# A graph network's first pass: gathered rows copied to PSUM by ScalarE, ends of edge lists found by one-hots, theta from rows in SBUF

## The chip, the cores and the metric

The kernel runs on one core of one Trainium2 chip. The metric is the time of one execution on the device in microseconds; of several runs the median is given. Engines are named as the profile names them: PE is TensorE's matmul and PEld its weight load, DVE is VectorE, ACT is ScalarE, POOL is GpSimd, SP is SyncE (here it only starts DMAs).

## The reference

Two graph layers with residuals and layer norms work on 6250 nodes of 256 features and 100000 edges, which are sorted by destination. All arithmetic is float32.

```python
def _L0_gnn_ref(x, src, dst, theta_w, theta_b, phi_w, phi_b):
    x_src = x[src]
    x_dst = x[dst]
    theta_x = (x_dst - x_src) @ theta_w.T + theta_b
    phi_x = x_src @ phi_w.T + phi_b
    e = jax.nn.relu(theta_x + phi_x)
    out = jax.ops.segment_max(e, dst, num_segments=x.shape[0])
    return jnp.where(jnp.isfinite(out), out, 0.0)

def _L1_gnn_ref(x, he, src, dst, W_in, b_in, W_u0, b_u0, W_u1, b_u1, W_ro, b_ro):
    hv = x @ W_in + b_in
    deg = jax.ops.segment_sum(jnp.ones_like(dst, jnp.float32), dst, num_segments=n)
    has_in = (deg > 0)[:, None]
    for W, b in ((W_u0, b_u0), (W_u1, b_u1)):
        m = jnp.concatenate([hv[src], he], axis=-1)
        m = jax.nn.relu(m @ W + b)
        msg = jax.ops.segment_max(m, dst, num_segments=n)
        hv = jnp.where(has_in, msg + hv, hv)
    return jax.nn.relu(hv @ W_ro + b_ro)

x = _layernorm(x + _L0_gnn_ref(x, src, dst, ...), axis=-1)
x = _layernorm(x + _L1_gnn_ref(x, edge_attr_64, src, dst, ...), axis=-1)
```

Since theta of a destination is the same for all its edges, the first layer needs the largest value of `x_src @ (phi - theta)` over a node's edges, to which theta of the node is added afterwards.

## The kernel before, in words

There are three passes over the edges: pass 0 is the first layer, passes 1 and 2 are the two rounds of the second. Each runs the same function `sweep(r)`. The edges, in reverse order of destination, are laid out as 14 blocks; in a block each of the 128 partitions (lanes) has 56 consecutive edges (54 in the last block), so a pass has 782 steps (`FS`), and one step takes one edge of each lane.

In a step GpSimd gathers 128 rows of 256 values from a table in HBM (`sources`, L790), 16 steps ahead of its use. In passes 1 and 2 TensorE adds the edge features (`pair`, L825) in PSUM, and VectorE adds the gathered rows to them, two steps at a time (L1030). VectorE then takes the running maximum along each lane (the scan, L1043): `cur = max(min(prev, lim), row)`, where `lim` is very negative at an edge that starts another destination. In pass 0 both inputs of the scan, `prev` and `row`, lie in SBUF, except in 40 steps (two of each eight in the first 160): for these, rows of x are gathered raw and multiplied on the core (`raw_turn`, `raw_pair`), and the scan reads PSUM. Every eight steps SP writes the scanned rows to a buffer `S` in HBM (L1051). At a block's end `over_lanes` carries the last row of each lane over to the lanes below (L836 to L857).

Nodes are handled in 49 tiles of 128, from the last to the first. `node(t, g, b)` puts a tile's work into slots, that is, behind given steps: at slot g GpSimd gathers the tile's rows from `S` by `end_i` (`rows`, L870), after the writes of `S` that were issued since the gather before it; at b-3 and b-2 VectorE and TensorE pick the rows that carry over (`picks` L882, `carried` L889, tile `v`); from b on come the additions, the layer norm, the products for the next table and the write of that table (pass 0: `first_a` to `first_g`, L904 to L928; later passes: `next_a` to `next_d` or `last_d` to `last_g`, L931 to L958). Which blocks a tile touches is fixed by `SPAN`, one to three blocks for each tile, 73 tile-block pairs in all.

All of this is one order written out by hand (`tc.manual_schedule()`): each engine takes its instructions in the order in which the code issues them, and waits on semaphores for the others. The slots only set that order. Tiles follow each other at a distance of `gap` slots, 6, 4 and 6 in the three passes.

Pass 0 has two more jobs before its nodes. `count` (L710 to L721) counts in-degrees: for each eight steps VectorE makes one-hot matrices `ol` and `oh` in bf16 (a single buffer each) and TensorE multiplies and sums them in PSUM (`hist`), one call every three steps from step 28 on. `ends_a` and `ends_b` turn the counts into `has` and `end_i`. So pass 0's first node gathers come at slot 324 and its first node steps at slot 344; after that a tile follows every six slots to slot 602, and the last five wait for their blocks. Theta is computed per tile at slots 8i+8 to 8i+21 (i = 0 for the last tile): SP loads the transposed rows (`x_in`, L894), TensorE multiplies (`theta`, L768 with `wt`), VectorE adds the bias and writes `h_sb` (`theta_out`, L900). The rows of x themselves are loaded to `x_sb` in seven DMAs at slots 160 to 208.

Of the kernel before, what the change touches and what calls it, by code (L numbers as in the profile page):

```python
# [17 lines left out]
P = 128  # L18
# [46 lines left out]
WIDE = max(sum(a <= b <= z for a, z in SPAN) for b in range(NB))  # L65

# [7 lines left out]
def gather_raw(nc, x, x_sb, s_r, i):  # L74

    nc.gpsimd.indirect_dma_start(out=x_sb[:, i, :], out_offset=None, in_=x,
                                 in_offset=bass.IndirectOffsetOnAxis(ap=s_r[:, i:i + 1], axis=0))
# [382 lines left out]
def gnn_kernel(  # L460
# [13 lines left out]
    above = const.tile([P, P], F32)  # L474
    nc.vector.tensor_scalar(above, jmp, 0.0, None, OP.is_gt)
# [4 lines left out]
    col = const.tile([P, P], BF16)  # L480
    nc.vector.tensor_copy(col, col_i)
# [30 lines left out]
    lo = const.tile([P, FS], BF16)  # L512
    hi = const.tile([P, FS], BF16)
    with tc.manual_schedule(), tc.tile_pool(name="pro", bufs=2) as pro, \
# [6 lines left out]
        for i in range(SOON):  # L521
            gather_raw(nc, x, x_sb, s_r, i)
        zero = pro.tile([1, D], F32, name="zero", bufs=1)
# [14 lines left out]
        def check():  # L538
# [15 lines left out]
            alike = BLOCKS.count(BLOCKS[0])  # L554
# [9 lines left out]
            nc.vector.tensor_scalar(bits, d_s, P - 1, None, OP.bitwise_and)  # L564
            nc.vector.tensor_copy(lo, bits)
            nc.vector.tensor_scalar(bits, d_s, 7, None, OP.arith_shift_right)
            nc.vector.tensor_copy(hi, bits)
# [29 lines left out]
def in_order(ctx: ExitStack, tc: tile.TileContext, g):  # L597
# [9 lines left out]
    table, ident, above, every, col, col_f = (g[n] for n in ("table", "ident", "above", "every", "col", "col_f"))  # L607
    whole, lim, lo, hi, s_s, fd, pd, ld, nd = (g[n] for n in ("whole", "lim", "lo", "hi", "s_s", "fd", "pd", "ld", "nd"))
    heT, xTn, xn, out = (g[n] for n in ("heT", "xTn", "xn", "out"))
    s_e, head, x, x_sb, wd, s_r = (g[n] for n in ("s_e", "head", "x", "x_sb", "wd", "s_r"))  # L610
    part = g["part"]
# [6 lines left out]
    has = one.tile([P, NT], F32, name="has")  # L618
# [3 lines left out]
    ones = one.tile([P, NT], F32, name="ones")  # L622
    nc.vector.memset(ones, 1.0)
# [72 lines left out]
    hist = psum.tile([P, 512], F32, tag="v", name="hist", bufs=1)  # L696

    none = one.tile([P, NT], BF16, name="none")
    nc.vector.memset(none, 0.0)
    half = (NG + 1) // 2  # L700
    low = []
    for i in range(2):
        low.append(psum.tile([P, 512], F32, tag="he", name="low", bufs=3))
        n = min(half * K, FS - i * half * K)
        nc.scalar.copy(low[i][:, :n], lo[:, i * half * K:i * half * K + n])

    def count(c):
        k = min(K, FS - c * K)
        ol = work.tile([P, K, P], BF16, name="ol", bufs=1)
        nc.vector.tensor_tensor(ol[:, :k, :], col.unsqueeze(1).to_broadcast([P, k, P]),  # L710
                                low[c // half][:, c % half * K:c % half * K + k].unsqueeze(2).to_broadcast([P, k, P]), OP.is_equal)
        b = max(i for i in range(NB) if FIRST[i] <= c * K)
        tiles = [t for t in range(NT) if SPAN[t][0] <= b <= SPAN[t][1]]
        t0, w = tiles[0], len(tiles)
        oh = work.tile([P, K, WIDE], BF16, name="oh", bufs=1)
        nc.vector.tensor_tensor(oh[:, :k, :w], col[:, t0:t0 + w].unsqueeze(1).to_broadcast([P, k, w]),  # L716
                                hi[:, c * K:c * K + k].unsqueeze(2).to_broadcast([P, k, w]), OP.is_equal)
        if c == 0:
            nc.tensor.matmul(hist[:, :NT], ol[:, 0, :], none, start=True, stop=False)
        for j in range(k):  # L720
            nc.tensor.matmul(hist[:, t0:t0 + w], ol[:, j, :], oh[:, j, :w], start=False,  # L721
                             stop=(c == NG - 1 and j == k - 1))

    cnt, incl, end = (one.tile([P, NT], F32, name=n) for n in ("cnt", "incl", "end"))
    sums = []

    def ends_a():
        nc.vector.tensor_copy(cnt, hist[:, :NT])
        ps = psum.tile([P, 512], F32, tag="pr", name="sums")
        nc.tensor.matmul(ps[:, :NT], above, cnt, start=True, stop=True)  # L730
        nc.tensor.matmul(ps[:, 64:64 + NT], every, cnt, start=True, stop=True)
        sums.append(ps)
        nc.vector.tensor_scalar(has, cnt, 0.0, None, OP.is_gt)

    def ends_b():
        lower, total = sums[0][:, :NT], sums[0][:, 64:64 + NT]
        nc.vector.tensor_tensor_scan(incl, ones, total, 0.0, OP.mult, OP.add)
        nc.vector.tensor_sub(end, total, incl)
        nc.vector.tensor_sub(end, end, lower)
        nc.vector.tensor_add(end, end, has)  # L740
        nc.vector.tensor_scalar(end, end, float(E - 2), 0.0, OP.add, OP.max)
        nc.vector.tensor_copy(end_i, end)
# [22 lines left out]
    def times(aT, w, n, tag="pr"):  # L765
        ps = psum.tile([P, 512], F32, tag=tag, name="prod", bufs=3 if tag == "he" else 2)
        for k in range(2):
            nc.tensor.matmul(ps[:, :n], aT[:, k, :], w[:, k, :], start=(k == 0), stop=(k == 1))  # L768
        return ps
# [349 lines left out]
```

## Time and profile before

| | |
|---|---|
| median of 6 runs | 4001.15 us (3986.94 to 4031.39) |
| the profiled execution | 4020.05 us |
| its span, first to last instruction | 4018.2 us |
| PE busy | 1875.5 us, 47% of the span |
| DVE busy | 2118.2 us, 53% |
| ACT busy | 238.1 us, 6% |
| POOL busy | 2390.3 us, 59% |
| mean granted TensorE clock | 0.684 |
| data moved over the span | 739.39 MB, 184 GB/s |

A group in the profile's tables reads: line, engine, operation, out<-in by the program's names, shapes, count, then after a bar the busy time and the mean duration in ns, and after the next bar the idle time of that engine just before the group and what ended most of it. "remote" is a wait whose end the profile cannot put down to an instruction, "issue" one that it cannot explain. A line of the waits has the engine and what it was about to do, whom it waited for, and then the total in us, the number of times and the longest.

### The profile page before, as it was taken

What the parts mean: (1) busy time and instruction counts of PE and PEld (TensorE: products, weight loads), DVE (VectorE), ACT (ScalarE), POOL (GpSimd) and SP (SyncE); (2) the same over time, 40 slices, a digit from 0 to 9 for tenths busy, and PEclk for the clock granted to TensorE, in tenths of its full rate; (3) what the DMA queues carried; (4) which work ended last, traced back from release to release, by engine and by line L of the source; (5) the groups of instructions that cost most, each with busy time, mean ns of one, the idle gap of its engine ahead of it and who ended that gap; (6) DMA issues with size and microseconds to landing.
All of it is one profiled execution on the core that took longest, in us unless ns stands there. A gap on an engine that the chain in (4) does not pass through costs nothing. (4 is left out here: it accounts for less than half of the span.)

```text
span 4018.2 us, 21650 instructions
## 1 busy us (share of the span) xinstructions
PE 1875.5 (47%) x4631; PEld 830.8 (21%) x4631; DVE 2118.2 (53%) x4750; ACT 238.1 (6%) x618; POOL 2390.3 (59%) x2500
## 2 busy tenths in 40 slices
PE   5552223555520354555445554455544544444455
PEld 4341111221200122222112211122222222111111
DVE  1465554554543355455445555445655655555555
ACT  1000001111100000000000000000000000000000
POOL 5456566666666565556655665655555556666663
PEclk8665556666555677777767767667777777777766
DMA  6456555555555565555555665555555555555554
GB/s 236 152 191 212 180 175 177 179 170 173 174 196 173 164 209 179 179 178 184 178 170 188 201 205 175 195 176 195 184 177 176 185 180 188 189 184 186 193 192 163
DMA packets 241821, 739.39 MB, mean 184 GB/s; under 512 B 52485, under 2 KB 95858, under 8 KB 204434
## 3 DMA queue, kind: packets, MB, share of 16 engines
q0 software_dynamic: 119664, 326.92, 27.3%
q1 hardware_dynamic: 69568, 337.85, 22.6%
q10 hardware_dynamic: 52450, 73.16, 5.5%
q8 instruction: 39, 0.64, 0.1%
q14 instruction: 100, 0.82, 0.1%
HBM read 404.56 MB, written 333.17 MB: 184 GB/s over the span
## 5 line engine op out<-in xcount | busy, mean ns | idle before, releaser
L790 POOL DMA_INDIRECT run<-table,s_s x2258 | 2163.4, 958 | 1258.1 <-issue 662.0
L825 PE MATMUL hp<-whe,hT 128*128 128x512 f32 x1564 | 1020.4, 750 | 802.0 <-DVE run L1043 391.5
L1043 DVE SCALAR_TENSOR_TENSOR run<-run,lim,hp 128x256 f32<-128x256 f32 x1573 | 753.8, 479 | 57.4 <-remote 10.7
L1030 DVE TENSOR_TENSOR hp<-hp,run 128x512 f32<-128x512 f32 x782 | 543.5, 695 | 366.4 <-remote 182.6
L825 PEld LDWEIGHTS hp<-whe,hT 128*128 128x128 f32 x1564 | 303.0, 225 | 1351.1 <-DVE run L1043 730.9
L1043 DVE SCALAR_TENSOR_TENSOR run<-run,lim 128x256 f32<-128x256 f32 x731 | 351.5, 481 | 153.8 <-remote 51.2
L870 POOL DMA_INDIRECT m<-S,end_i x147 | 141.4, 962 | 312.8 <-DMA S<-run 208.0
L889 PE MATMUL v<-cs,pick 128*128 128x256 f32 (+1 forms) x438 | 167.2, 502 | 156.8 <-issue 54.6
L931 DVE TENSOR_TENSOR m<-m,v 128x256 f32<-128x256 f32 x98 | 40.6, 414 | 328.5 <-remote 207.0
L768 PE MATMUL prod<-wcat,aT 128*128 128x512 f32 x196 | 176.6, 1054 | 55.2 <-issue 41.6
L710 DVE TENSOR_TENSOR ol<-col,low 128x1024 bf16<-128x1024 bf16 x98 | 118.8, 1213 | 104.6 <-remote 85.8
L721 PE MATMUL hist<-oh,ol 128*128 128x8 bf16 (+7 forms) x782 | 34.8, 167 | 279.0 <-DVE oh L716 184.5
L768 PE MATMUL prod<-wro,aT 128*128 128x256 f32 x196 | 81.4, 556 | 170.2 <-ACT aT L762 89.8
L889 PEld LDWEIGHTS v<-cs,pick 128*128 128x128 f32 x438 | 102.2, 253 | 265.9 <-issue 211.6
L947 DVE TENSOR_TENSOR m<-prod,bro 128x256 f32<-128x256 f32 x49 | 20.8, 425 | 234.5 <-remote 103.9
L768 PE MATMUL prod<-wu,aT 128*128 128x256 f32 x196 | 74.4, 516 | 117.8 <-issue 88.5
L760 PE MATMUL tp<-ident,x_sb 128*128 128x128 f32 x98 | 32.1, 429 | 158.3 <-DVE x_sb L755 68.3
L760 PE MATMUL tp<-ident,h_sb 128*128 128x128 f32 x196 | 48.3, 335 | 121.6 <-DVE h_sb L935 50.1
L926 DVE TENSOR_TENSOR new<-prod,b 128x256 f32<-128x256 f32 x49 | 20.8, 424 | 156.1 <-PE prod L768 89.0
L932 ACT ACTIVATE m<-m,has 128x256 f32<-128x256 f32 x98 | 49.7, 507 | 865.5 <-DVE m L931 368.0
L721 PEld LDWEIGHTS <-ol 128*128 128x128 bf16 x782 | 36.3, 104 | 304.6 <-DVE ol L710 214.9
L762 ACT COPY aT<-tp 128x256 f32<-128x256 f32 x147 | 54.7, 372 | 742.4 <-remote 309.4
(131 smaller groups left out, 1389.0 us busy)
## 6 DMA issues: line engine op xcount, KB each, us to landing
S<-run SPq DMA_DIRECT2D x291, 1024.0 KB
hT<-in_heT ACTq DMA_DIRECT2D x196, 256.0 KB
run<-table,s_s POOLq DMA_INDIRECT x2258
table<-new ACTq DMA_DIRECT2D x98, 128.0 KB
xg<-in_xTn SPq DMA_DIRECT2D x7, 896.0 KB
xT<-in_xTn SPq DMA_DIRECT2D x49, 128.0 KB
x_sb<-in_xn SPq DMA_DIRECT2D x7, 896.0 KB
out<-new ACTq DMA_DIRECT2D x48, 128.0 KB
```

Of the source, the lines that this page charges most:

```text
L710: nc.vector.tensor_tensor(ol[:, :k, :], col.unsqueeze(1).to_broadcast([P, k, P]), low[c // half][:, c % half * K:c % half * K + k].unsquee ...
L721: nc.tensor.matmul(hist[:, t0:t0 + w], ol[:, j, :], oh[:, j, :w], start=False, stop=(c == NG - 1 and j == k - 1))
L760: nc.tensor.transpose(tp[:, k * P:(k + 1) * P], a[:, k * P:(k + 1) * P], ident)
L762: nc.scalar.copy(aT.rearrange("p k e -> p (k e)"), tp[:, :2 * P])
L768: nc.tensor.matmul(ps[:, :n], aT[:, k, :], w[:, k, :], start=(k == 0), stop=(k == 1))
L790: nc.gpsimd.indirect_dma_start(out=runs[s // K][:, s % K, :], out_offset=None, in_=table[r][:SPARE + 1, :] if early else table[r], in_offs ...
L825: nc.tensor.matmul(hp[i], hT[c][:, q, :], whe[r - 1].rearrange("p s f -> p (s f)"), start=True, stop=not early)
L870: i = nc.gpsimd.indirect_dma_start(out=o["m"], out_offset=None, in_=S_r[:P * (FIRST[SPAN[t][1]] + BLOCKS[SPAN[t][1]]), :], in_offset=bass. ...
L889: nc.tensor.matmul(o["v"][:, :N1], p, cs[:, blk % KEPT, :N1], start=(blk == SPAN[t][0]), stop=(blk == SPAN[t][1]))
L932: nc.scalar.activation(o["m"], o["m"], AF.Relu, scale=has[:, t:t + 1])
L1030: nc.vector.tensor_add(sums, sums, two)
L1043: nc.vector.scalar_tensor_tensor(cur, prev, lim[:, s:s + 1], row, OP.min, OP.max)
```

## The change

Pass 0 is changed in four ways, and the later passes in one.

- Each pair of gathered rows is copied by ScalarE into a PSUM buffer (`bring`, three buffers with tag "he", which theta and the copies for counting used before), two pairs ahead of the scan; the scan reads its row from PSUM in all steps. The raw rows' products go to the same buffers.
- In-degrees are no longer counted. `ends(t)` finds for each tile, at slot g-12, which lane of which block holds the node's last edge (two VectorE steps make a one-hot over lanes and nodes for each tile-block pair, TensorE multiplies it with the lanes' destinations in `lane`), and VectorE counts in PSUM how many of the lane's edges precede. From that come `end_i`, and `keeps`, which takes the place of `has`: very large for a node with edges and very negative for one without.
- Theta is no longer computed ahead into `h_sb`. A tile's rows in `x_sb` are transposed (`x_turn`, slot b-6) and multiplied (`theta`, b-4); the bias is added by one more matmul with the identity, and the sum is read from PSUM in `first_b`. The seven loads of `x_sb` come at slots 2 to 138, and the raw rows are stored in `x_sb` in reverse, so that the places are free in time.
- With no counting to wait for, nodes begin as soon as their block is scanned: the first tile's rows are gathered at slot 56 and its steps begin at slot 76. The distance in pass 0 is 8 slots.
- In all passes, adding, cutting off below zero and masking are two fused VectorE steps or one, where VectorE and ScalarE took turns before, and the later steps of a node follow one or two slots earlier.

```diff
 def gather_raw(nc, x, x_sb, s_r, i):
-    nc.gpsimd.indirect_dma_start(out=x_sb[:, i, :], out_offset=None, in_=x,
+    nc.gpsimd.indirect_dma_start(out=x_sb[:, RAW - 1 - i, :], out_offset=None, in_=x,
...
+        nc.gpsimd.iota(n_i, pattern=[[P, NT]], base=1, channel_multiplier=1)
+        nc.gpsimd.iota(at_i[:, :alike], pattern=[[P * BLOCKS[0], alike]], base=-1, channel_multiplier=BLOCKS[0])
...
-            nc.vector.tensor_scalar(bits, d_s, P - 1, None, OP.bitwise_and)
-            nc.vector.tensor_copy(lo, bits)
-            nc.vector.tensor_scalar(bits, d_s, 7, None, OP.arith_shift_right)
-            nc.vector.tensor_copy(hi, bits)
+            nc.vector.tensor_copy(n1, n_i)
+            nc.vector.tensor_copy(fn[:, 0, :], fd)
+            nc.vector.tensor_copy(fn[:, 1, :], nd)
+            nc.vector.tensor_copy(lane[:, :, BLOCKS[0]:], at_i.unsqueeze(2))
...
-    def count(c):
...
-    def ends_a():
...
-    def ends_b():
...
+    def ends(t):
+        b0, b1 = SPAN[t]
+        top = work.tile([P, NB], F32, name="top")
+        nc.vector.tensor_scalar(top[:, b0:b1 + 1], fn[:, 0, b0:b1 + 1], float(-P * t), None, OP.add)
+        ps = psum.tile([P, 512], F32, tag="tp", name="ends")
+        for b in range(b0, b1 + 1):
+            own = work.tile([P, P], F32, tag="pick", name="here", bufs=4)
+            nc.vector.tensor_scalar(own, col_f, fn[:, 1, b:b + 1], float(-P * t), OP.subtract, OP.is_gt)
+            nc.vector.scalar_tensor_tensor(own, col_f, top[:, b:b + 1], own, OP.is_le, OP.mult)
+            nc.tensor.matmul(ps[:, :BLOCKS[0] + 1], own, lane[:, b, :], start=b == b0, stop=b == b1)
+        found = work.tile([P, 2, BLOCKS[0]], F32, name="found")
+        num = work.tile([P, 2], F32, name="num")
+        for i, op in enumerate((OP.is_ge, OP.is_equal)):
+            nc.vector.scalar_tensor_tensor(found[:, i, :], ps[:, :BLOCKS[0]], n1[:, t:t + 1], every[:, :BLOCKS[0]], op,
+                                           OP.mult, accum_out=num[:, i:i + 1])
+        nc.vector.tensor_scalar(end_i[:, t:t + 1], ps[:, BLOCKS[0]:BLOCKS[0] + 1], num[:, 0:1], 0.0, OP.add, OP.max)
+        nc.vector.tensor_scalar(keeps[:, t:t + 1], num[:, 1:2], 0.0, 2.0 * BIG, OP.is_gt, OP.mult)
+        nc.vector.tensor_scalar(keeps[:, t:t + 1], keeps[:, t:t + 1], -BIG, None, OP.add)
...
-    def times(aT, w, n, tag="pr"):
+    def times(aT, w, n, more=None):
...
+        if more is not None:
+            nc.tensor.matmul(ps[:, :n], ident, more, start=False, stop=True)
...
-        def raw_pair(i):
-            aT = rT.pop(i)
-            hp[i * K // 2] = psum.tile([P, 512], F32, tag="pr", name="hp")
+        def bring(i):
+            hp[i] = psum.tile([P, 512], F32, tag="he", name="hp", bufs=3)
+            if raw(2 * i) is None:
+                c, q = divmod(i, K // 2)
+                nc.scalar.copy(hp[i], runs[c][:, 2 * q:2 * q + 2, :].rearrange("p s f -> p (s f)"))
+                return
+            aT = rT.pop(raw(2 * i) // 2)
...
-            def x_in():
-                o["xT"] = work.tile([P, K // 2, P], F32, tag="hT", name="xT", bufs=4)[:, :2, :]
-                nc.sync.dma_start(o["xT"], xTn[:, :, t * P:(t + 1) * P])
+            def x_turn():
+                o["xT"] = turned(x_sb[:, t, :])
             def theta():
-                o["h"] = times(o["xT"], th, D, tag="he")
-            def theta_out():
-                nc.vector.tensor_add(h_sb[:, t, :], o["h"][:, :D], tb)
+                o["h"] = times(o["xT"], th, D, more=tb)
...
             def first_b():
-                nc.vector.tensor_add(o["m"], o["m"], h_sb[:, t, :])
-                nc.scalar.activation(o["m"], o["m"], AF.Relu, scale=has[:, t:t + 1])
-            def first_c():
-                nc.vector.tensor_add(o["m"], o["m"], x_sb[:, t, :])
+                nc.vector.scalar_tensor_tensor(o["m"], o["m"], keeps[:, t:t + 1], o["h"][:, :D], OP.min, OP.add)
+                nc.vector.scalar_tensor_tensor(o["m"], o["m"], 0.0, x_sb[:, t, :], OP.max, OP.add)
...
             def next_a():
-                nc.vector.tensor_max(o["m"], o["m"], o["v"][:, :D])
-                nc.scalar.activation(o["m"], o["m"], AF.Relu, scale=has[:, t:t + 1])
+                nc.vector.scalar_tensor_tensor(o["m"], o["m"], keeps[:, t:t + 1], o["v"][:, :D], OP.min, OP.max)
...
             if r == 0:
-                i = NT - 1 - t
-                at(8 * i + 8, x_in)
-                at(8 * i + 20, theta)
-                at(8 * i + 21, theta_out)
+                at(max(2, g - 12), ends, t)
+                at(b - 6, x_turn)
+                at(b - 4, theta)
...
-                for i, f in ((0, first_a), (1, first_b), (3, first_c), (4, first_d), (6, first_e), (7, first_f),
-                             (9, first_g)):
+                for i, f in ((0, first_a), (1, first_b), (2, first_d), (4, first_e), (5, first_f), (7, first_g)):
...
-                for i, f in ((0, next_a), (2, next_b), (3, next_c)):
+                for i, f in ((0, next_a), (0, next_b), (1, next_c)):
...
-            for c in range(NG):
-                at(3 * c + 28, count, c)
-            begin = 3 * NG + 30
-            at(begin - 2, ends_a)
-            at(begin - 1, ends_b)
-        gap = (6, 4, 6)[r]
+        gap = (8, 4, 6)[r]
...
+                    if s == 0:
+                        bring(1)
+                    if s + 4 < FS:
+                        bring(s // 2 + 2)
                     sums = hp.pop(s // 2)
```

## The prediction

> **What bounds the kernel now.** I read the page first, then a table of busy time by stretch, then VectorE's groups and GpSimd's waits inside the stretches of pass 0. The cuts come from the scan instructions in order of time (one per step): step 0 starts at 97.5 us, step 616 at 1121.7, step 781 ends at 1350.6; passes 1 and 2 run to 2683 and 4018. The span is 4018.2 us, the execution 4020.05, so 1.9 us lie around it.
>
> ```profile
> core 0: us, PE busy (x) PEld busy (x) DVE busy (x) ACT busy (x) POOL busy (x), PEclk, DMA share, GB/s
> ...
> 97.00:604.00 507.00, 184.95 (x1215) 136.87 (x1214) 290.99 (x584) 14.87 (x34) 282.72 (x292) 0.56 0.55 182
> 604.00:1121.00 517.00, 258.88 (x457) 104.84 (x456) 260.64 (x769) 72.43 (x194) 329.19 (x336) 0.61 0.52 172
> 1121.00:1350.00 229.00, 31.19 (x53) 12.57 (x53) 92.17 (x212) 8.09 (x25) 156.16 (x158) 0.52 0.55 185
> ```
>
> I call these stretches I (counting, theta, raw rows), II (most nodes) and III (the rest). No engine is over 68% busy, so waits set the pace. The firm floor is GpSimd: a gather is 0.95 us busy and 0.30 us of issue, 1.25 us. Stretch III is near it: 158 gathers x 1.25 = 198 of 229 us. In I and II it is 292 + 336 = 628 gathers, 785 of 1024 us: 239 us are lost to something else. VectorE's rows say what:
>
> ```profile
> L710 DVE TENSOR_TENSOR ol<-col,low 128x1024 bf16<-128x1024 bf16 x97 | 117.9, 1215 | 104.6 <-remote 85.8 <-issue 11.4 <-PE hist L721 5.5
> ...
> L900 DVE TENSOR_TENSOR h_sb<-prod,tb 128x256 f32<-128x256 f32 x38 | 16.1, 423 | 66.1 <-PE prod L768 32.2 <-remote 26.6 <-issue 5.1
> ```
> ```profile
> L926 DVE TENSOR_TENSOR new<-prod,b 128x256 f32<-128x256 f32 x44 | 18.7, 425 | 144.6 <-PE prod L768 81.3 <-remote 48.3 <-issue 14.9
> ...
> L900 DVE TENSOR_TENSOR h_sb<-prod,tb 128x256 f32<-128x256 f32 x11 | 4.6, 422 | 29.0 <-remote 24.2 <-PE prod L768 2.2 <-PE v L889 1.9
> ```
>
> The first fence is stretch I, the second stretch II; the number after the second bar is VectorE's idle time just before the group. VectorE stood 104.6 us before the counting one-hots (their single buffer is still read by TensorE), 95.1 us before theta's add, 144.6 us before `new`, always for TensorE. GpSimd's waits show that this reaches the gathers:
>
> ```profile
> POOL run L790 <- DVE run L1043: 84.4, 11, 22.7
> POOL run L790 <- issue: 83.6, 266, 2.1
> POOL run L790 <- PE hist L721: 24.8, 2, 14.2
> ```
> ```profile
> POOL m L870 <- DMA S<-run: 74.9, 12, 14.4
> ```
>
> Stretch I: gathers wait for buffers that the scan has not given back (84.4 + 24.8 us). Stretch II: the gather of S rows waits for writes of S that come after late scans (74.9 us). So in I and II VectorE's program order, with TensorE's answers in it, ends last. That is the place the change touches.
>
> **What is removed** (VectorE, I + II). Counting: 118.8 us in 98 wide one-hots, 19.3 in the narrow ones (L716), 104.6 idle. Theta's add: 49 x 0.42 = 20.7 busy, 95.1 idle. Together 358.5 us. If VectorE's order sets the pace throughout, 1024 falls to 665.5. Part of the removed idle would only move, so the additions below are counted as idle too.
>
> **What is added** (about 45 of the 49 nodes fall into I + II).
> - `ends`, work: two 128x128 one-hot steps for each of 73 tile-block pairs at the pick's 0.295 us = 43 us; for each tile `top`, `end_i` and two `keeps` at 0.15, two PSUM reductions at 0.19 (the 128x49 rows) = 49 us. Together 92, of which 90 here.
> - `ends`, wait: it reads its matmul in the same task, so VectorE stops and the scans queued behind it stop with it. No row shows this matmul. Low end 0.5 us (the wait before the lane scan, L845: 4.7 us over 10 in I); high end 3.3 us (L926: 144.6 / 44, behind TensorE's queue). I take 1.0, as only small matmuls stand just ahead: 47 us.
> - Theta moves from its own slots to between a node's transposes and its `wcat` product: slot b-4 of one node is slot (b-8)+4 of the node before. Four matmuls and two for the bias at about 0.4 us each (41 took 16.6 us) = 2.4 us, of which ScalarE's copy of `aT` (0.37) covers a part: 2.0 us more before `new`, 44 x 2.0 = 88. Low end 0, if VectorE's own work covers it; high end 178, twice that. The two transposes for it come two slots earlier: nothing, while TensorE has a gap.
> - `v` now follows `wcat` in TensorE's queue: 0.54 us x 2 x 1.5 less a scan of 0.48, some 0.7 us a node: 31. Ends 0 and 62.
> - Two fused steps at 0.48 for two adds at 0.42: 5 us. ScalarE's 0.51 us relu goes; its result was used two slots later, so this frees nothing.
>
> Sum for I + II: 665 + 90 + 5 + 47 + 88 + 31 = 926 us, above the gathers' 785. Saving 98.
>
> **ScalarE's copies.** 371 copies of 128x512; the nearest row takes 0.586 us (L800, out of PSUM). 217 us over 1250 on an engine busy 95 us there: hidden. The new wait is that each copy stands in ScalarE's order until two gathers have landed and a PSUM buffer is free; behind it queue `aT`, `sd`, the issue of `table<-new`, and VectorE waits for those. It is issued four steps ahead and gathers run 16 ahead, so I count nothing; without that cover, rival three. The scan reading PSUM costs no more: 478 ns against 483 (stretch I, L1043). What it can win is contention with GpSimd: the gather takes 989 ns in III and 949 in pass 2, where the scan reads PSUM; 53 scans in III waited 41.7 us for the scan before them, which the rows of passes 1 and 2 do not show. On the gathers' path that is 158 x 0.04 = 6 us, bounded by 0 and the 31 us that III lies above its floor; I take 8, since the other stops of III are waits for S.
>
> The Trainium skill, "SBUF — State Buffer", section on the two separate sides, says that VectorE and GpSimd share a port pair that one of them holds exclusively, and that a VectorE step with two SBUF inputs takes it only against a GpSimd step that reads SBUF; whether a gather counts as one it does not say. By it the whole 27 ns between pass 0's mean (975) and pass 2's would go, 784 x 0.027 = 21 us.
>
> **Nothing counted.** Three iotas join GpSimd's queue in the prologue (0.12 to 0.23 us in its timeline). SP loses 49 loads of xT (6.3 MB); its seven loads of x's rows move from steps 160-208 to 2-138, ahead of S writes. An 896 KB load at the mean 184 GB/s is 5 us, and the DMA engines are 55% busy: up to 35 us if each stood on the path. The prologue swaps four 782-wide steps for a few. Passes 1 and 2 lose ScalarE's relu and get a 0.48 step for a 0.41 one: +6 us at most, and 0.5 us less in each tail. I count none.
>
> Sum: 4020 - 98 - 8 = 3914 for the profiled execution, which is 19 us above the median of the runs (4001). Against the median 3895, and I round to 3900.
>
> TensorE's granted clock was 0.56 and 0.61 in I and II. The Trainium skill, "TensorE: Matmul & The Clock Gate", part 1, has a busier TensorE run at twice the idle rate; by it theta's 2.0 us would be 1.0 and the sum 44 us lower. The row speaks against leaning on it: II has more matmul work than I and hardly a higher clock.
>
> **Rivals.**
> 1. The floor takes over (0.2). If VectorE's remaining waits fall under the gathers, I + II end at 785 plus the 75 + 10 us of waits for S that II shows: 870, a saving of 154; with all of III's 31, 4001 - 185 = 3816. For it: VectorE's lag behind a gather is elastic by 16 steps. Against it: the 144.6 us before `new` stay.
> 2. Slower: TensorE's queue (0.22). In II there are spells in which TensorE answers late: around 647 and 658 us VectorE stood 9.99 and 9.86 us before L900 and L926, and 13.8 before the next `new`. Theta, its transposes and `ends` now stand in that same queue for every node, before `wcat`. It decides from 8 us a node: 45 x 8 = 360, what was removed; `ends` and the fused steps use 2.1 of it. If six nodes in ten pay 10 us and the others 3.7, that is 45 x 7.5 = 338: 665 + 95 + 338 = 1098, 74 above 1024, and 4001 + 74 - 8 = 4067. Against it: only six waits of `new` in 44 were of that kind.
> 3. No difference (0.10): ScalarE's order holds the scans. If at each node the copies for the next pairs come 2 us late behind `aT` and `h_sb`, 45 x 2 = 90 of my 106 are lost: 3985.
> The forecast itself has 0.48, with 3850 to 3940 from half of theta's ends either way.
>
> **Range and chances.** From 3815 (rival 1) to 4060 (the `ends` wait at 3.3 us, +104, and half of theta's upper end, +45, give 3895 + 149 = 4044; rival 2's 4067 is just beyond). 0.5% (20 us) is about what a measurement can tell from no change. Faster: 0.46 of the forecast and 0.2 of rival 1, 0.66. Same: 0.10. Slower: 0.24, rival 2 and the forecast's upper tail.
>
> **What would show it.** Right: step 616 is reached some 98 us earlier after step 0; no VectorE wait for hist or L900; the idle before `new` rises from 3.3 to about 5 us; `ends` shows about 1 us a tile before its first reduction; gathers in pass 0 near 0.95 us; passes 1 and 2 within 10 us of 1333 and 1335. Wrong: VectorE waiting long for ScalarE's copies; waits for TensorE of 8 us a node; gathers of S waiting more than the 85 us of II; or a pass 1 or 2 that changes by more than 20 us.

## The result, and the profile after

The changed kernel takes 4060.43 us (median of 20 runs, 4039.11 to 4085.18) where the kernel before, in the same comparison, takes 4011.28 us (46 runs, 3975.85 to 4044.41). The ratio is 1.0122, 95% interval 1.0103 to 1.0142: it is slower, by 49 us. The profiled execution took 4051.19 us, 31 us more than the one of before.

From the scan instructions in order of time, in us:

| | before | after |
|---|---|---|
| step 0 | 97.5 | 101.4 |
| steps 0 to 324 (I) | 507 | 548 |
| steps 324 to 616 (II) | 517 | 506 |
| step 616 to the end of 781 (III) | 229 | 234 |
| pass 1, steps 0 to 781 | 1303 | 1285 |
| pass 2, steps 0 to 781 | 1299 | 1310 |

So pass 0 lost 35 us. The differences of passes 1 and 2 are not told apart from scatter: another pair of profiles has 1287 and 1285, 1300 and 1319, so pass 2 was longer in both pairs; but the version with the removed work left out (below), whose later passes are those of before, has 1293 and 1311 on another chip. The table of busy time by stretch, after:

```profile
core 0: us, PE busy (x) PEld busy (x) DVE busy (x) ACT busy (x) POOL busy (x), PEclk, DMA share, GB/s
101.00:650.00 549.00, 255.72 (x784) 169.62 (x782) 271.70 (x909) 125.65 (x281) 297.78 (x314) 0.70 0.49 168
650.00:1156.00 506.00, 150.00 (x387) 91.65 (x387) 222.00 (x693) 108.97 (x236) 295.04 (x312) 0.62 0.48 162
1156.00:1390.00 234.00, 44.87 (x103) 25.13 (x103) 97.61 (x250) 53.41 (x106) 152.78 (x161) 0.53 0.55 186
```

VectorE's busy time in I + II is 494 us (272 + 222), where it was 552: about as the sum had it. Its idle time rose instead. VectorE's groups in I + II (the number after the second bar is the idle time just before the group):

```profile
L1011 DVE SCALAR_TENSOR_TENSOR run<-run,lim,hp 128x256 f32<-128x256 f32 x606 | 287.7, 475 | 83.8 <-remote 41.2 <-issue 17.6 <-ACT hp L786 2.4
L715 DVE SCALAR_TENSOR_TENSOR found<-ends,n,every 128x56 f32<-128x56 f32 x92 | 21.7, 274 | 73.3 <-remote 35.7 <-PE ends L711 25.3 <-issue 10.7
L903 DVE TENSOR_TENSOR new<-prod,b 128x256 f32<-128x256 f32 x44 | 18.7, 425 | 288.0 <-remote 170.9 <-PE prod L745 98.7 <-issue 18.4
...
L884 DVE TENSOR_SCALAR no<-v 128x1 f32<-128x1 f32 x44 | 6.8, 154 | 67.7 <-remote 49.6 <-issue 11.9 <-PE v L873 6.1
```

The 104.6 us before `ol` and the 95.1 before theta's add are gone. In their place there are 288.0 us before `new` (144.6 before the change), 73.3 before the ends' first reduction, 67.7 before `v` is read (11.6 before). Most of it is called remote. For ScalarE's copies the scans wait 2.4 us. GpSimd's waits in the same stretch:

```profile
POOL run L769 <- issue: 177.8, 552, 3.5
POOL m L854 <- DMA S<-run: 163.5, 19, 16.1
POOL run L769 <- DMA S<-run: 64.9, 9, 14.7
POOL m L854 <- DVE here L710: 20.4, 1, 20.4
```

Of the waits for the scan to give back `run` 12.3 us are left, of those for `hist` nothing. Nearly all of GpSimd's lost time but the issue is now a wait for writes of S (228 us) and one long wait for the first tile's ends. Of these 228, 64.9 us are gathers that need a `run` buffer whose write to S has not landed (18.1 before). The gathers of S rows (L854) waited 201.3 us, issue included; in stretch II of before it was 87.

### The profile page after: what moved, and what is told of

Read it like the earlier page. It is cut to its first block, busy times and chain, and to the rows that moved or that the text cites. A ratio compares the mean times of both kernels' runs of the same rounds, so it can differ in the third digit from the quotient of the medians.

```text
span 4049.4 us, 21930 instructions
## 1 busy us (share of the span) xinstructions
PE 1844.6 (46%) x4186; PEld 872.0 (22%) x4186; DVE 2080.8 (51%) x5034; ACT 381.0 (9%) x889; POOL 2368.7 (58%) x2503
## 5 line engine op out<-in xcount | busy, mean ns | idle before, releaser
L1011 DVE SCALAR_TENSOR_TENSOR run<-run,lim,hp 128x256 f32<-128x256 f32 x2304 | 1100.8, 478 | 184.3 <-remote 46.3
L809 PE MATMUL hp<-whe,hT 128*128 128x512 f32 x1564 | 991.4, 733 | 387.7 <-DVE run L1011 223.6
L854 POOL DMA_INDIRECT m<-S,end_i x147 | 139.4, 948 | 423.2 <-DMA S<-run 332.6
L786 ACT COPY hp<-run 128x512 f32<-128x512 f32 x371 | 218.9, 591 | 467.9 <-issue 199.3
L737 PE MATMUL tp<-ident,x_sb 128*128 128x128 f32 x196 | 55.0, 376 | 425.6 <-DVE x_sb L732 212.8
L908 DVE SCALAR_TENSOR_TENSOR m<-m,keeps,v 128x256 f32<-128x256 f32 x98 | 46.7, 476 | 347.8 <-remote 301.5
L739 ACT COPY aT<-tp 128x256 f32<-128x256 f32 x196 | 72.3, 369 | 1588.7 <-remote 679.8
L737 PEld LDWEIGHTS tp<-ident,h_sb 128*128 128x128 f32 x196 | 24.1, 171 | 603.8 <-issue 481.5
L745 PE MATMUL prod<-wcat,aT 128*128 128x512 f32 x196 | 133.8, 820 | 17.3 <-ACT aT L739 10.6
L919 DVE TENSOR_TENSOR new<-prod,bu 128x256 f32<-128x256 f32 x49 | 20.8, 425 | 228.7 <-issue 97.7
L737 PEld LDWEIGHTS tp<-ident,x_sb 128*128 128x128 f32 x196 | 31.1, 200 | 440.7 <-issue 409.5
L745 PE MATMUL prod<-wt,aT 128*128 128x256 f32 x196 | 93.1, 628 | 71.8 <-issue 39.2
```

The source lines that it names most:

```text
L737: nc.tensor.transpose(tp[:, k * P:(k + 1) * P], a[:, k * P:(k + 1) * P], ident)
L739: nc.scalar.copy(aT.rearrange("p k e -> p (k e)"), tp[:, :2 * P])
L786: nc.scalar.copy(hp[i], runs[c][:, 2 * q:2 * q + 2, :].rearrange("p s f -> p (s f)"))
L809: nc.tensor.matmul(hp[i], hT[c][:, q, :], whe[r - 1].rearrange("p s f -> p (s f)"), start=True, stop=not early)
L854: i = nc.gpsimd.indirect_dma_start(out=o["m"], out_offset=None, in_=S_r[:P * (FIRST[SPAN[t][1]] + BLOCKS[SPAN[t][1]]), :], in_offset=bass. ...
L908: nc.vector.scalar_tensor_tensor(o["m"], o["m"], keeps[:, t:t + 1], o["v"][:, :D], OP.min, OP.max)
```

## The experiments

Four theories. **Q**: TensorE's queue; theta, its transposes and the ends' matmuls stand ahead of `wcat`, so VectorE waits. **A**: ScalarE's copies hold its other work and the scans. **P**: a phase. S is written at steps 7, 15, 23 and so on, and a tile's rows of S are gathered at slot g behind all writes issued so far. Before, tiles came every 6 slots, so g fell right behind a write once in four tiles; now they come 8 slots apart from slot 56 on, or wait for the end of a block of 56 steps, so that g is a multiple of 8 for all tiles but the last, and each gather stands one step behind a write. **S**: TensorE answers late in spells; whatever VectorE reads next waits, and the price does not go with the work that is removed.

All ratios are to the kernel before on the same chip. The first four of the runs (copies, theta, ends and S gathers, one part each) were on a chip on which the kernel before takes 3221.55 us; all others were on chips on which it takes 4011 to 4053, as in the comparison.

### The changed kernel and the one before, again

> The changed kernel as it is. On the chip of the first four experiments the kernel before took 3221.6 us where it took 4011 in the comparison, and the waits that the profile calls remote (VectorE and ScalarE behind late answers of TensorE) are gone there: passes 1 and 2 take 1026 and 1029 us. Theory S (late spells: the loss of 1.2% is the price of more waits for TensorE in a chip that answers late in spells): without spells the ratio to before is 0.985 to 1.003, and pass 0 about 1020 us. Theory Q (the order in TensorE's queue costs by itself): 1.010 to 1.020, whatever the chip.

> The kernel before, for its profile on this chip. Theory S: VectorE's 104.6, 95.1 and 144.6 us of idle time ahead of ol, theta's add and new shrink together to under 200, since a part of them was spells; so less was to be removed than the 200 us I took from the rows. Theory Q: they stay within a fifth.

> The changed kernel as it is, since two kinds of chip have turned up: one on which the kernel before takes 4011 to 4015 us and the trace has late answers of TensorE (1.2% loss, pass 0 1253 to 1288 and 1301 us), and one on which it takes 3222 us and has none. Theory S (late answers make the loss): on a chip without them the ratio is 0.995 to 1.003; on one with them 1.010 to 1.016. Theory Q (queue order by itself): 1.010 to 1.016 on both.

> The changed kernel as it is, to stand beside the others of this call on the same chip. On a chip with late answers 1.010 to 1.020; on one without, theory S 0.995 to 1.003, theory Q 1.010 to 1.016.

Measured: 1.0143 (1.0116 to 1.0170), 1.0180 (1.0116 to 1.0244) and 1.0155 (1.0065 to 1.0245). All three chips were of the 4000 us kind, so the loss stands, and what the unedited change does on the other kind was not seen. The second profile of before agrees with the first within a fifth (115, 84 and 161 us before `ol`, theta's add and `new`), so theory S's expectation of less to remove, meant for the other chip, was not tried by it.

### One part taken back

Without ScalarE's copies (`bring` returns without copying, the scan reads `runs`):

```diff
-                nc.scalar.copy(hp[i], runs[c][:, 2 * q:2 * q + 2, :].rearrange("p s f -> p (s f)"))
...
-                    sums = hp.pop(s // 2)
+                    sums = hp.pop(s // 2) if raw(s) is not None else runs[c][:, j:j + 2, :].rearrange("p s f -> p (s f)")
```

> Scans read the gathered rows where they landed in SBUF, as before the change; ScalarE's 371 copies are gone, raw rows still come in PSUM. Reference points: changed kernel 4060 us, pass 0 1288 us from step 0 to step 781; before 4001 to 4011, 1253. Theory Q (TensorE's queue: theta, its transposes and the ends' matmuls stand ahead of wcat, so VectorE waits 288 us ahead of `new` and 68 ahead of `v`): copies cost nothing, time within 10 us of the changed kernel, or 5 to 20 us slower by contention (gathers from 0.949 back to 0.975 us). Theory A (copies in ScalarE's order hold aT, sd and the scans): 40 to 90 us faster, VectorE's idle time ahead of the scans (104 us in steps 0 to 616) falls below 40. Theory P (gathers of S rows stand right behind the S write, since nodes now come every 8 steps and S is written every 8 steps): within 10 us.

> ScalarE's copies alone taken back. On a chip with late answers: with theta taken back as well the time fell from 1.0143 to 1.0029 of before. If the copies made that (theory A), this run has 1.000 to 1.006 and the scans' idle time falls; if theta did (theory Q), 1.010 to 1.016. On a chip without late answers: 1.001 as measured before.

Theta as before (its loads, two matmuls on the old slots, VectorE's add into `h_sb`):

```diff
...
-                at(b - 6, x_turn)
-                at(b - 4, theta)
+                i = NT - 1 - t
+                at(8 * i + 8, x_in)
+                at(8 * i + 20, theta)
+                at(8 * i + 21, theta_out)
```

> Theta as before the change: xT loaded from HBM, two matmuls per tile on a fixed order of every 8 steps from step 20, bias added by VectorE into h_sb; all else as changed. Theory Q: TensorE loses eight instructions ahead of each `wcat`; idle ahead of `new` falls from 6.5 to about 3.5 us a node (131 us less over 44), VectorE pays 49 x 0.42 = 21 us for the add plus its waits; pass 0 falls by 50 to 110 us, time 3950 to 4010. Theory A: within 15 us of 4060. Theory P: within 25 us of 4060, since the gathers of S rows still stand 200 us.

> Theta alone taken back. On a chip with late answers: theory Q gives 0.998 to 1.005, with the idle time ahead of `new` at 120 to 160 us in steps 0 to 616 instead of 288 and 302; theory A gives 1.010 to 1.016. On a chip without them: 1.002 as measured before.

Both of these together:

> Changed kernel with both theta as before (loads of xT, two matmuls each on their own steps, an add by VectorE) and scans from SBUF without ScalarE's copies: what is left of the change is ends by one-hots, nodes from step 76 every 8 steps, and the fused steps. By my sum counting's 243 us go and 142 come: 90 to 110 us faster than before if VectorE's order sets the pace. Theory Q: the gain shows (ratio 0.97 or less), as theta no longer stands ahead of wcat. Theory F (GpSimd's floor of 1.25 us a step and the waits for S set the pace in pass 0 on this chip): within 0.5% of before.

Measured, on the 3222 us chip: 1.0012 (1.0002 to 1.0021) without copies, 1.0022 (1.0012 to 1.0033) with early theta. On the others: 1.0122 (1.0057 to 1.0187) and 1.0094 (1.0060 to 1.0128) beside the changed kernel's 1.0180 (1.0116 to 1.0244), and 1.0029 (1.0005 to 1.0053) for both, beside 1.0143. With early theta the idle time before `new` fell from 299 us in the changed kernel on that chip to 150.1, as theory Q had it, and before `v` from 60 to 37.1. The time fell by only 35 us by the ratios, 21 by the medians; the idle time before scans took up a part (81 to 115 us). The copies are worth 24 by the ratios and 21 by the medians. The intervals of the ratios overlap, but all runs of the two variants (at most 4105.64 us) are faster than all four of the changed kernel on that chip (at least 4108.06). With both taken back most of the loss is gone, but the gain of 90 to 110 us that my sum had for ends and nodes alone is not there: in place of the waits for `ol` VectorE has 127 us before scans (53 in the kernel before) and 60 before `found`. GpSimd in that run:

```profile
POOL run L769 <- issue: 165.4, 543, 0.3
POOL m L852 <- DMA S<-run: 158.4, 18, 15.9
POOL run L769 <- DMA S<-run: 38.7, 4, 14.8
```

So ends in place of counting brought nothing as long as the gathers of S rows wait like this (theory F of the expectation: within 0.5% of before); what they bring without that wait the last version below shows in part.

### More slack for the readers

Ends read two steps behind their matmul:

```diff
-        ps = psum.tile([P, 512], F32, tag="tp", name="ends")
+        ps = psum.tile([P, 512], F32, tag="v", name="ends", bufs=1)
...
-                at(max(2, g - 12), ends, t)
...
+                at(max(2, g - 12), look)
+                at(max(2, g - 12) + 2, look_out)
```

The ends' sum thereby moves to the PSUM buffer of `v`, out of those of the transposes, so this is not the two steps alone.

> The two reductions that read the ends' matmul stand two steps behind it instead of in the same task; nothing else changes. Theory Q: the 73 us of idle time ahead of the first reduction fall below 25; pass 0 falls by 20 to 50 us, time 4010 to 4040. Theories A and P: the wait moves to the next thing late (scans, `new`), time within 12 us of 4060.

> Ends read two steps behind their matmul, nothing else. Together with the later gathers of S rows it took pass 0 from 1301 to 1252 us on a chip with late answers. If the wait inside the ends' task made half of that or more (my term of 47 us, measured 73), 0.995 to 1.007 there; if the gathers of S rows made it (theory P), within 0.5% of the changed kernel of this call. Without late answers 0.994 as before, and 0.5 to 0.8% below the changed kernel.

Gathers of S rows six steps later in pass 0:

```diff
-            at(g, rows)
+            at(g + 6 if r == 0 and t else g, rows)
```

> In pass 0 the gather of S rows for a node stands six steps later in GpSimd's order (g + 6 instead of g), so that the last write of S ahead of it is seven steps old instead of one; b, where VectorE uses the row, stays 14 steps behind. Theory P: GpSimd's idle time ahead of these gathers falls from 201 us to under 60, pass 0 by 60 to 110 us, time 3950 to 4000. Theory Q: GpSimd waits only because VectorE is late; the wait shifts to other places (gathers waiting for `run`), pass 0 within 20 us of 1288.

> Gathers of S rows six steps later in pass 0, nothing else. Theory P (each of them stands one step behind a write of S, since 8 steps lie between nodes and between writes): on a chip with late answers 0.998 to 1.006, GpSimd's idle time ahead of them from 200 to under 120 us; otherwise within 0.5% of the changed kernel. Without late answers 0.998 as before.

> Both edits that helped alone: ends read two steps behind their matmul (0.9944 of before alone) and gathers of S rows six steps later (0.9983 alone). If they remove different waits the ratio is 0.986 to 0.992; if both only free the same lead of the gathers, 0.993 to 0.996.

Measured: the split ends gave 0.9944 (0.9928 to 0.9961) on the 3222 us chip and 1.0106 (1.0018 to 1.0195) beside the changed kernel's 1.0155; the wait before `found` fell from 82.0 to 39.3 us there. The later gathers gave 0.9983 (0.9973 to 0.9992) and 1.0038 (1.0007 to 1.0068), beside the same 1.0155: 48 us between the medians, 4075.34 and 4027.06. Both together gave 1.0034 (1.0009 to 1.0058) beside 1.0143: no more than the gathers alone. GpSimd's waits over steps 0 to 616 with the later gathers:

```profile
POOL run L769 <- issue: 168.4, 544, 1.7
POOL run L769 <- DMA S<-run: 109.5, 14, 14.4
POOL m L854 <- DMA S<-run: 107.0, 20, 15.0
POOL run L769 <- DVE run L1011: 24.1, 12, 15.7
```

On that chip the changed kernel has 200.9 us in the third of these rows and 72.3 in the second:

```profile
POOL m L854 <- DMA S<-run: 200.9, 23, 20.8
...
POOL run L769 <- DMA S<-run: 72.3, 13, 14.6
```

A part of the wait moved to gathers that need the `run` buffer back, and 36 us of steps 0 to 616 were won (1063 to 1027). VectorE's wait before `new` stayed at 279.9 us. TensorE's queue is untouched in this run, so these 48 us hang on where the gathers of S stand, as theory P has it.

The traces bear this out and limit it. In the two profiles of before, GpSimd stood 3.1 us on average ahead of a pass 0 gather of S right behind a write, 2.0 to 2.6 ahead of those three or five steps behind, and 0.5 to 0.6 seven steps behind. In the four profiles of the changed kernel 48 of the 49 stand right behind, at 4.4 to 4.7 us each; six steps later it is 2.8. On the 3222 us chip the same place costs little: in the variant without copies 0.8 us a gather there, 4.4 on the other kind. So the place costs much only where the writes of S come late. No run has a distance other than 8.

All kinds of slack at once, in all passes; each gather of S waits only for the writes that it reads:

```diff
-                for w in pending:
+                need = [w for w in pending if w[0] < FIRST[SPAN[t][1]] + BLOCKS[SPAN[t][1]]]
+                for _, w in need:
...
-            at(g, rows)
+            at(g + 6 if t else g, rows)
...
-                for i, f in ((0, first_a), (1, first_b), (2, first_d), (4, first_e), (5, first_f), (7, first_g)):
+                for i, f in ((0, first_a), (1, first_b), (2, first_d), (4, first_e), (5, first_f), (10, first_g)):
```

> The changed kernel with more slack at four places: ends read two steps behind their matmul; `new` read ten steps behind b instead of seven; gathers of S rows six steps later, in all passes, and waiting only for the writes of S rows that they read, not for the latest write. Theory S (late answers are only harmful where a reader stands right behind): on a chip with late answers GpSimd's idle time ahead of gathers of S rows in pass 0 falls from 200 to under 90 us and the time to 0.970 to 0.995 of before; without them 0.985 to 0.995. Theory Q: TensorE's work ahead of wcat is the same, the time stays above 1.003 where answers are late.

The same later, narrowed gathers in the kernel before:

> The kernel before with the later gathers of S rows alone (six steps later in all passes, waiting only for the writes that they read). GpSimd waits 208 us for writes of S at these gathers in the whole of before. If that wait is on the path by itself (theory P), 0.970 to 0.990 and this beats the changed kernel with the same edit (0.993); if VectorE behind TensorE is what is late (theory S), the wait moves to gathers that wait for `run`: 0.992 to 1.003.

Measured: 0.9928 (0.9897 to 0.9959), and 0.9908 (0.9870 to 0.9946) for the kernel before with the gathers alone. VectorE's rows of the first of the two:

```profile
L906 DVE TENSOR_TENSOR new<-prod,b 128x256 f32<-128x256 f32 x44 | 18.4, 418 | 9.8 <-PE prod L747 8.3 <-issue 1.5
...
L887 DVE TENSOR_SCALAR no<-v 128x1 f32<-128x1 f32 x44 | 7.0, 158 | 243.8 <-remote 123.9 <-PE v L876 91.1 <-PE prod L747 8.8
```

The changed kernel on the same chip has 299 us before `new` and 60 before `v`. In this version, which reads `new` three steps later, 290 us of idle time are gone before it, and 184 came back before the next thing that VectorE reads from TensorE: a wait that only changed its place. The kernel before gained nothing in pass 0 (1255 us, 1253 without the edit), where GpSimd's 75 us at gathers of S turned into more waits for `run`:

```profile
POOL run L790 <- issue: 168.6, 545, 1.9
POOL run L790 <- DVE run L1044: 123.3, 17, 22.5
POOL run L790 <- DMA S<-run: 57.5, 15, 13.7
POOL run L790 <- PE hist L721: 24.5, 2, 13.8
```

In the profiles passes 1 and 2 have 1277 and 1280 us, where two of before have 1303 and 1299, 1287 and 1300: by these profiles that is where the edit pays. So the wait for S was not what held up pass 0 before the change; after it, the same wait cost 48 us.

### The removed work left out

> The kernel before with the work that the change removes simply left out: no counting one-hots and matmuls, no theta (its loads, matmuls and adds); the S rows that the nodes take are then fixed ones and x stands for theta's result, all other instructions stay. It measures the 358.5 us that I took as removed from VectorE's order. If VectorE's order sets the pace throughout (my sum), steps 0 to 616 fall from 1024 us to the gathers' 785 to 870, ratio 0.935 to 0.960. If only GpSimd's own waits for a late VectorE or TensorE count (84 + 25 us in stretch I), 0.970 to 0.980. If the 137 us of the removed idle time that the rows put down to remote are spells of TensorE that meet whatever VectorE reads next (theory S), and VectorE's busy time is covered by the gathers, 0.980 to 1.000, with the idle time coming back ahead of the scans and of new.

```diff
-                at(3 * c + 28, count, c)
...
-                at(8 * i + 8, x_in)
-                at(8 * i + 20, theta)
-                at(8 * i + 21, theta_out)
```

Measured: 0.9792 (0.9718 to 0.9866), 81 us between the medians. The ratio lies in the second of the three ranges, and its interval reaches into the third; the first, my sum, is out. That is all that the removed work was worth, against the 358.5 us of my sum, in the order of the kernel before, where nodes still begin at slot 344. In the profile stretch I fell from 507 to 403 us, near GpSimd's own 84 + 25 us of waits there, and stretch II rose from 517 to 536. VectorE's waits over steps 0 to 616:

```profile
DVE run L1040 <- remote: 108.4, 25, 21.1
DVE new L926 <- PE prod L768: 73.1, 26, 7.6
DVE run L1040 <- DMA run<-table,s_s: 70.9, 48, 4.5
```

Before, the scans had 27.6 us of remote waits and 4.5 for the gathers' landing. With `ol` and theta's add gone the scans are what VectorE reads next, and the remote waits are theirs. 200 us of idle time were taken out, and VectorE's idle time over these steps went from 472 to 517 us.

### The version that the runs point to

> The version that the runs point to: ends by one-hots, read two steps behind their matmul, and the fused steps are kept; theta and the scans' operands are taken back to before; gathers of S rows six steps later in all passes, waiting only for the writes that they read. The changed kernel with the slack alone had 0.993, before with the later gathers alone 0.991, theta and copies taken back gained 0.011 on the changed kernel. If these overlap, since all of them only give lead back to the gathers, 0.985 to 0.993; if they add, 0.975 to 0.985.

Measured: 0.9879 (0.9797 to 0.9960), 3963.70 us against 4011.51. It beats both kernels; that it beats the kernel before with the later gathers (0.9908) is not shown, since the intervals overlap. Pass 0 took 1217 us in its profile, 36 less than the two profiles of before; the other versions with all of the work are at 1252 to 1309 on such chips. The ratio lies in the range given for gains that overlap. In pass 0 of the profiles they nearly add: 1301 us in the changed kernel, 1254 with theta and copies taken back, 1217 with the slack as well; these are single profiles, on two chips.

## Why the prediction was wrong

It forecast 3900 us and faster; it came to 4060.43 and slower, just beyond the upper end of the range, 4060. That the range comes so near is luck: its upper end rests on an ends' wait of 3.3 us a tile, and 1.6 was measured.

**The step that failed** is the base of the sum: "Together 358.5 us. If VectorE's order sets the pace throughout, 1024 falls to 665.5." Left out alone, that work was worth 81 us. Two things were mis-sized in it. First, whether the 158.8 us of busy time lay on the path is not told by VectorE's rows, but by who waited for it: GpSimd's waits in stretch I, 84.4 and 24.8 us, were shown beside them, and stretch I gave 104 us when the work was left out. Second, the idle time. The shown row has 85.8 of `ol`'s 104.6 us as remote, and the two rows of theta's add have 26.6 and 24.2: 137 of 200 us the profile could not put down to the work that stood there. Over steps 0 to 616 VectorE's remote waits were 238 and 240 us in two profiles of before, 306, 266, 288 and 247 in four of the changed kernel, 202 with theta and copies taken back, 185 without counting and theta: a fifth to three tenths of the stretch, whichever work stands in it.

**Additions.** By the removed work's 81 us and the loss of 49, they cost some 130 us, where I had 260 on VectorE's order; both sides were too large, and the removed side by more. One by one: the ends' wait, 47 us predicted, measured 73.3 (split, it gave 20 us between medians, with wide intervals). Theta and `v`, 88 + 31 = 119 us predicted, measured 143 + 56 = 199 more idle time before `new` and `v`, but theta taken back gave 21 to 35 us. The term for `v` does not follow from its factors: 0.54 x 2 x 1.5 less 0.48 is 1.14 us a node, not 0.7, so 50 us, not 31, and the sum 945. Theta's six matmuls took TensorE 2.9 us a node (83.0 + 44.9 us over 44), not 2.4. VectorE's work, a change of -64 us by my terms, measured -58. Copies, nothing counted: 2.4 us of waits before scans; taken back, 21 us between medians.

**The term that was missing** is the place of the S gathers. Rival 1's "waits for S that II shows", 75 + 10 us, were carried over as they stood, and the sum has no term for them. The new distance of 8 slots was in the diff and S is written every 8 steps; moving the gathers six steps on gave 48 us, the size of the whole loss. It is not the only edit that does so: theta and the copies taken back together gave 40 us between medians, with the gathers left where they were.

**Rival 2** gave 4067 us and so named the time. In VectorE's rows it came near: 11 remote waits before `new` took 170.9 us, and the idle time added before `new`, `v` and the ends' reduction is 143 + 56 + 73 = 272 us, where it had 338. But it priced these rows one for one, as the forecast did. Theta taken out of TensorE's queue took 149 us away from before `new` and gave 21 to 35 us; and the edit that gave 48 us leaves the queue as it is. So the number fits by errors that cancel: added waits and removed work were both priced too high. Rival 3 had 90 us lost to the copies; 21 were measured, and 2.4 us of waits before scans. Rival 1, the gathers' floor, was not reached.

**The list.** Step 616 came 30 us later, not 98 earlier. The wait before `new` is 6.5 us, not 5; the ends' 1.6 a tile, not 1. Passes 1 and 2, counted to the end of each, took 1313 and 1347 us, where 1333 and 1335 within 10 were expected. Gathers are 0.949 us, as said. S gathers wait 201 us, which was on the list of what would make it wrong. III was to save 8 us and lost 5: the gathers' 40 ns came, but they were not what ended last there.

On the two rules: on the 3222 us chip the gathers of pass 0 took 971 ns with scans from SBUF and 950 with scans from PSUM.

```profile
L769 POOL DMA_INDIRECT run<-table,s_s x727 | 705.9, 971 | 221.6 <-issue 194.5 <-DMA run<-table,s_s 11.9 <-DVE run L1009 5.2
```
```profile
L769 POOL DMA_INDIRECT run<-table,s_s x730 | 693.8, 950 | 224.5 <-issue 199.4 <-DMA run<-table,s_s 8.2 <-DVE run L1011 5.5
```

The prediction left open whether a gather counts in the rule of the Trainium skill, "SBUF — State Buffer", section on the two separate sides, by which 27 ns would go: these rows fit it, with 21 ns, though no run shows that the port is the reason. The rule of "TensorE: Matmul & The Clock Gate", part 1, that a busier TensorE runs faster, agrees with the granted clock of stretch I (0.70 after, 0.56 before). Theta's matmuls did not gain, 628 ns after and 602 before; those of `wcat`, which now follow them in TensorE's queue, did, 820 ns after and 1054 before. Stretch II speaks neither way: 150 us of TensorE work after, 259 before, and a clock of 0.62 and 0.61.

**Open**: what makes TensorE late, what each added term costs by itself, and the unedited change on a chip without late answers. There its four variants with one part altered were between 0.994 and 1.002, so the loss of 1.2% is not likely there, but that was not run.

## What to carry to other kernels

An idle row says what the engine was about to read, not what its wait is worth. Before idle time is counted as removed, look whether the releaser is the work that goes ("PE hist") or something that will meet the next reader ("remote"), and take the saving from the waits of the engine that paces the loop, not from the rows of the one ahead of it. And when a distance in a fixed order is changed, compare it with the periods of what it waits for: a gather every 8 slots beside a write every 8 steps is always at the same place, here right behind the write, where it waits longest.

## What the runs showed of the hardware

Chips differ by a fifth on the same program. On four chips the kernel before took 4011 to 4053 us, on one 3221.55 (3217.43 to 3226.38 over 25 runs). A gather takes 949 and 951 ns on the two kinds, a scan 478 on both (the changed kernel, and the one with later S gathers); what is gone is the waits called remote, of which the trace there has none. ScalarE's read of TensorE's transposes, in the page of the kernel before and in that of the variant with early theta on the 3222 us chip:

```profile
L762 ACT COPY aT<-tp 128x256 f32<-128x256 f32 x147 | 54.7, 372 | 742.4 <-remote 309.4
```
```profile
L739 ACT COPY aT<-tp 128x256 f32<-128x256 f32 x147 | 54.7, 372 | 1077.1 <-PE tp L737 927.2
```

The copy began more than 2 us after the start of the last transpose in 32 of 147 cases in the first, by 10.5 us at the ninth decile, and in 1 of 147 in the second; the second's kernel on a chip of the first kind has 22 of 147 and 9.2 us. Passes 1 and 2 take about 1026 us there, 1.31 us a step, and most of GpSimd's remaining idle time is issue (438 us over both with the later S gathers). The recorded clock is 0.5 or 1.0 of full speed on both; on the 4000 us chips the half-speed stretches often last 14 to 31 us, on the other mostly 3 to 7. Whether the long stretches make the late answers or follow from them is not shown.
